# A two-layer image kernel: transposed scan output and norm in the first layer, transposed softplus and folded convolution in the second

## Chip, cores and metric

The kernel runs on one core of one Trainium2 chip. The time is the device time of one execution in microseconds (us); lower is better. The engines are named as the profile names them: PE (TensorE, matrix products; PEld is its loading of weights), DVE (VectorE), ACT (ScalarE), POOL (GpSimd) and SP (SyncE, which here only issues DMAs). Each engine works through its own queue in order. All data is float32.

## The reference, cut to what matters

The input is x of shape (8, 192, 64, 64). Layer 0 is a gated two-dimensional scan, layer 1 a pair of selective state-space scans over 4096 tokens.

```python
# layer 0
x = conv1x1(x, W_in)                                  # 192 -> 384 channels
x = depthwise_conv3x3(x, W_dw) + b_dw
x_proxy = conv1x1(x, W_xd)                            # 16 channels
ws, Ls, Us, Ds = (conv1x1(x_proxy, W) for W in (W_w, W_l, W_u, W_d))
xs = the image, its transpose, and both with the last axis flipped     # 4 directions
Gl, Gm, Gr = normalize_w(*split(ws, 3))               # each / (|Gl| + |Gm| + |Gr| + 1e-7)
# gate_scan, chunks of 8 columns, step j within a chunk:
#   h = l * x + gl * h_up + gm * h + gr * h_down
out = gate_scan(xs, Ls, Gl, Gm, Gr, 8) * Us + xs * Ds
y = sum over the 4 directions of out * w_m
y = layernorm2d(y, ln_w, ln_b)                        # over the 384 channels
y = grn(y, grn_gamma, grn_beta)                       # global response norm
x = conv1x1(y, W_out)                                 # 384 -> 192

# layer 1: xs = layernorm of x seen as (b, 4096, 192); out = xs + mamba1(xs) + mamba2(xs flipped)
xc, z = split(x @ in_w.T)                             # 384 each
xc = silu(causal_conv4(xc, conv_w) + conv_b)
dt, B, C = split(xc @ x_w.T)                          # 12, 16, 16
dt = softplus(dt @ dt_w.T + dt_b)
# over the tokens:  h = exp(dt * A) * h + dt * x * B ;  y = sum over 16 states of h * C
y = (y + D * xc) * silu(z)
return y @ out_w.T
```

## The kernel before

One core holds 128 partitions, so the 384 inner channels are three blocks (c = 0, 1, 2). Everything is unrolled, and the order in which the program issues its parts is the order of each engine's queue (`tc.manual_schedule`). The program is 512 columns wide in nearly all operations.

**Layer 0** (`tile_ss2d_kernel`) takes the 8 images one after the other. Per image:

- 24 *units* (`Image.begin`, L137, and `unit`, L188): one channel block by eight image rows. PE multiplies with W_in, ACT writes the middle tap with the bias and two side taps, POOL adds the two sides (L162), and DVE adds the six other taps (L196).
- `proxy` (L173) makes the 16-channel proxy of eight rows for the gates.
- 96 *steps* (`Step`), 3 blocks x 8 j x 4 directions d, in `scan` (L347). A step's parts run over several steps of the loop (L361 to L385), which issues parts of the steps s3, s2, s1, s0 and of the one ahead. PE makes the gates with 16 rows of contraction (L237): lam, gl, gm and gr in `gates`, and the pair of bypass and output gates in `up` (L305). DVE forms three products with the neighbours' state (`neighbour`, L263), the sum of magnitudes (`norm`, L278), two operations that refine a reciprocal made by ACT (`newton`, L294 and L295), the weighting (`mix`, L299) and the output product (`output`, L319): nine operations. POOL multiplies the entry (L257), adds a pair (L267), makes the state (L303) and multiplies the bypass dx (L313). PE adds q's terms through an identity (L273), and adds hu and dx of all four directions into one bank, yp, through an identity (`add`, L321, matmul L329). For direction 2 dx is not added by PE: POOL adds it to the dx of direction 3 (L315). After direction 3, ACT stores yp (L339). For j = 0 the state is the entry product alone, so that a step has only entry, bypass and output.
- The y of an image lies with channels on the partitions, 512 positions to a column block j. `Norm` (L388) of the image before is issued between the first units: means over the channels by a product with a constant matrix (L399), centring on DVE (L404), squares on ACT (L408), a second product (L413), an inverse root with three DVE refinements (L419 to L423), scaling on POOL (L442), and the squares' sums for the response norm on ACT (L430).
- `project_out` (L460) multiplies with W_out in 16 products (L499), spread over the later units by the list PARTS, and stores to DRAM (mid).

PSUM banks of layer 0 come from `bank` (L62): one each for gl, gm, q and yp, two for gr, two for c. The gates lam, bypass and output all take c; a tile that finds no free one waits for the last reader of an earlier one.

**Layer 1** (`tile_mamba_kernel`) has 64 blocks of 512 tokens, two *passes* for each (the two mambas), 128 in all. A pass has 24 *groups*: three channel blocks by eight pairs of states. For a group:

- `inputs` (L861): POOL multiplies dtx with the pair's rows of B, which a DMA has spread over the partitions (b_sb), into hs.
- `decays` (L867): ACT writes exp(dt * a) into a PSUM pair da, twice, and the first column of hs (L870).
- `scan` (L875): DVE runs the recurrence over 1024 columns.
- `weigh` (L882): the product with C (c_sb). DVE does it, except for *far* groups, n in FAR, whose scan is written to hs and whose product is POOL's.
- `keep` (L878): ACT saves the last state; `sum` (L887): PE adds both states' products, transposed, into yp with 8 matmuls in transpose mode.

The loop over slots (L984 to L1009) issues, at slot n: what `before[n]` lists, the inputs of group n + 3, scan n, far product n - 1, sums of n - 3 (far: n - 4), product and keep of n, decays of n + 2, and what `behind[n]` lists. The lists are made by L907 to L947. They hold the next pass's preparation: in_proj into xr (`enter`, L683), the convolution by four diagonal matrices (`convolve`, L700), z by `gate` (L712), `silu` (L721), `low_rank` (L727), the write of B and C to DRAM (bc, L735) and their 16 spread loads (`spread`, L743). `step` (L746) makes the softplus in six ACT operations with channels on the partitions; `refine` (L763) finishes it on POOL with three operations and forms dtx with a fourth (L766, L768, L770, L773); `head` makes the first column. Banks of layer 1: two for all preparation, two for yp, and two pairs for da. hs has 10 buffers, b_sb and c_sb eight each.

Of the kernel before, what the change touches and what calls it, by code (L numbers as in the profile page):

```python
# [8 lines left out]
F32 = mybir.dt.float32  # L9
# [22 lines left out]
FAR = (0, 12, 15, 20)  # L32
ACT_SET = "natural_log_exp_and_others"
JOINED = 2
UNITS = NC * CHUNK

PARTS = [0] * 8 + [1, 1, 1, 2, 1, 1, 1, 1, 1, 1, 1, 1, 1, 1, 1, 1]
# [4 lines left out]
ROWS = {GL: (0, 0), GM: (1, 0), GR: (2, 0), GLAM: (3, 0), GU: (0, 1), GD: (1, 1)}  # L42


@with_exitstack
def kernel(ctx: ExitStack, tc: tile.TileContext, x, w_in, dw, vecs, w_xd, w_gate, w_m, w_out, mid):
# [9 lines left out]
    big = ctx.enter_context(tc.tile_pool(name="l0_big", bufs=6))  # L56
# [46 lines left out]

    states = []
# [8 lines left out]
    class Image:  # L113
# [6 lines left out]
        def __init__(self, b):  # L120
            self.b = b
            self.x = x[b].rearrange("(k p) h w -> p k (h w)", p=KM)
            self.xc, self.xins, self.banks = [], {}, {}
            self.xp = p1.tile([P, CHUNK, CHUNK, HW], F32, tag="xp", name=f"xp_{b}")
            self.u = 0
            for u in range(4):
                self.load(u)
            for u in range(2):
                self.begin(u)
# [7 lines left out]
        def begin(self, u):  # L137
            c, r = divmod(u, CHUNK)
            if r == 0:
                self.xc.append(big.tile([P, HW, HW], F32, tag="big", name=f"xc_{self.b}_{c}"))  # L140
# [5 lines left out]
            self.load(u + 4)  # L146
# [26 lines left out]
        def proxy(self, r):  # L173
            pp = bank("c", f"pp_{self.b}_{r}")
# [13 lines left out]
        def unit(self):  # L188

            u, self.u = self.u, self.u + 1  # L190
            if u + 2 < UNITS:
                self.begin(u + 2)
            c = u // CHUNK
            for t in (0, 1, 2, 6, 7, 8):
                acc, part = self.shifted(u, t)
                nc.vector.scalar_tensor_tensor(  # L196
                    acc, part(self.banks[u]), dw_sb[:, c, t : t + 1], acc, ALU.mult, ALU.add
                )
            if u >= UNITS - CHUNK + 2:
                self.proxy(u % CHUNK - 2)  # L200
# [17 lines left out]
    class Step:  # L218
# [4 lines left out]
        def __init__(self, tag, xc, xp, wg, d, j):  # L223
            self.tag, self.xc, self.xp, self.wg, self.d, self.j = tag, xc, xp, wg, d, j
            self.q, self.ab = {}, {}
            self.h = states[d]
            self.hc = self.h[:, :, 1 : HW + 1]
# [4 lines left out]
        def gate(self, kind, tag):  # L232

            dst = bank(tag, f"g{kind}_{self.tag}")
            group, at = ROWS[kind]
            r = slice(32 * group, 32 * group + RANK)
            nc.tensor.matmul(dst, self.wg[r, at, self.d, :], flat(self.xp[r, self.j]), start=True, stop=True)  # L237
            return dst
# [36 lines left out]
        def norm(self):  # L275
            if self.j:
                for i in range(2):
                    nc.vector.tensor_add(self.g[2], self.g[2], flat(self.ab[i]))  # L278
# [11 lines left out]
        def newton(self):  # L290

            if self.j:
                s, rc = self.g[2], flat(self.rc)
                nc.vector.scalar_tensor_tensor(s, s, 1e-7, rc, ALU.add, ALU.mult)  # L294
                nc.vector.scalar_tensor_tensor(rc, s, 2.0, rc, ALU.subtract, ALU.mult)  # L295
# [25 lines left out]
        def add(self, i):  # L321


            if self.d == 0 and i == 0:
                self.yp = bank("yp", f"yp_{self.tag}")
            elif i == 0:
                self.yp = self.before.yp
            if i == 0 or self.d != JOINED:
                nc.tensor.matmul(  # L329
                    self.yp,  # L330
                    ident,
                    flat((self.hu, self.dx)[i]),
                    start=(self.d == 0 and i == 0),
                    stop=(self.d == ND - 1 and i == 1),
# [6 lines left out]
    class Nothing:  # L341


        def __getattr__(self, part):
            return lambda *args: None

    def scan(b, xc, xp):  # L347


        ys, steps = [], [Nothing()] * 4  # L350
        for c in range(NC):
            wg = w_gate_sb[:, :, :, c * P : (c + 1) * P]
            ys.append(big.tile([P, CHUNK, CHUNK * HW], F32, tag="big", name=f"y_{b}_{c}"))
            for j in range(CHUNK):
                steps += [Step(f"{b}_{c}_{j}_{d}", xc[c], xp, wg, d, j) for d in range(ND)]
                for step in steps[-ND:]:
                    step.y = ys[c][:, j, :]
        for before, step in zip(steps[4:], steps[5:]):
            step.before = before
        steps += [Nothing()] * 4  # L360
        for s3, s2, s1, s0, ahead in zip(steps, steps[1:], steps[2:], steps[3:], steps[4:]):  # L361
            s2.state()
            s0.neighbour(2)
            s0.neighbour(0)
            s0.entry()
            s1.newton()
            s1.total()
            s0.neighbour(1)
            s0.pair()
            s0.magnitude(2)  # L370
            s2.direct()
            ahead.gates()
            s0.norm()
            s0.log()
            ahead.decay()
            s2.bypass()
            s3.add(0)
            s2.output()
            s3.add(1)
            ahead.magnitude(0)  # L380
            s1.up()
            s0.exp()
            s1.mix()
            ahead.magnitude(1)
            s3.store()  # L385
        return ys

    class Norm:  # L388


        def __init__(self, b, ys):
            self.b, self.ys = b, ys
            self.ss = p1.tile([P, NC, CHUNK], F32, tag="ss", name=f"ss_{b}")
            self.pm, self.squares, self.var, self.rstd = {}, {}, {}, {}

        def mean(self, j):
            self.pm[j] = bank("gr", f"pm_{self.b}_{j}")
            for c in range(NC):
                nc.tensor.matmul(self.pm[j], mean_w, self.ys[c][:, j, :], start=(c == 0), stop=(c == NC - 1))  # L399

        def center(self, j):
            for c in range(NC):
                y = self.ys[c][:, j, :]
                nc.vector.tensor_sub(y, y, self.pm[j])  # L404
                sq = self.squares[j, c] = p2.tile(
                    [P, T], F32, tag=("ab0", "ab1", "dx")[c], name=f"sq_{self.b}_{j}_{c}"
                )
                nc.scalar.activation(sq, y, AF.Square)  # L408

        def variance(self, j):  # L410
            self.var[j] = bank("c", f"pv_{self.b}_{j}")
            for c in range(NC):
                nc.tensor.matmul(self.var[j], mean_w, self.squares[j, c], start=(c == 0), stop=(c == NC - 1))  # L413

        def root(self, j):

            r = self.rstd[j] = p2.tile([P, T], F32, tag="rc", bufs=3, name=f"rstd_{self.b}_{j}")
            v = self.var[j]
            nc.scalar.activation(r, v, AF.Ln, bias=eps5)  # L419
            nc.scalar.activation(r, r, AF.Exp, scale=-0.5)  # L420
            nc.vector.scalar_tensor_tensor(v, v, 1e-5, r, ALU.add, ALU.mult)
            nc.vector.tensor_mul(v, v, r)
# [665 lines left out]
```

## Time and profile before

| | us |
|---|---|
| median of 3 runs | 16998.98 (16979.7 to 17001.8) |
| the profiled execution, its own time | 16973.27 |
| its span, first to last instruction | 16971.4 |
| busy: PE | 14236.2 (84%) |
| busy: DVE | 15279.7 (90%) |
| busy: ACT | 12149.0 (72%) |
| busy: POOL | 15186.0 (89%) |

An engine is busy while one of its instructions runs; matmuls overlap, so a full PE row says that the queue never ran dry, not that the array was at its peak. The profile cuts the span into 40 slices of 424 us. Layer 0 fills the first 14 of them. The costliest groups are POOL's inputs (7157.5 us in 3072 instructions of 2357 ns) and DVE's scans (5852.3 and 1168.8 us, 2286 ns each).

### The profile page before, as it was taken

The page shows a single profiled execution, that of the slowest core. Times are in us where ns is not written, and L with a number is a line of the kernel's source. Part 1 is how long each engine was busy: PE and PEld are TensorE (multiplying, and loading weights), DVE is VectorE, ACT ScalarE, POOL GpSimd, SP SyncE. Part 2 cuts the span into 40 slices and gives each one's busy share as a digit, 9 for nine tenths or more (in the row PEclk, how much of TensorE's full clock was granted, in tenths as well). Part 3 has the DMA queues.
Part 4 walks back from the last instruction along what each step waited for, and adds up shares of the span by engine and source line. Part 5 has one row for each costly group of instructions (what it writes and reads, how often), then busy time and mean ns, then how long its engine had stood idle before and what let it go on. Part 6 is the DMA issues. An engine that isn't in the chain of part 4 may idle for free.

```text
span 16971.4 us, 183983 instructions
## 1 busy us (share of the span) xinstructions
PE 14236.2 (84%) x58320; PEld 7740.8 (46%) x58320; DVE 15279.7 (90%) x14474; ACT 12149.0 (72%) x25963; POOL 15186.0 (89%) x9955
## 2 busy tenths in 40 slices
PE   9999999999999977777777777777777777777777
PEld 2333333333333345555555555555555555555555
DVE  8888888888887779999999999999999999999999
ACT  5656666666666667777777777777777777777777
POOL 7787978778787779999999999999999999999999
PEclk8999999999999988888888888888888888888888
DMA  1001010010100022222222222222222222222222
GB/s 30 24 7 30 1 30 8 23 30 1 30 1 26 2 96 105 105 105 105 104 106 104 106 104 106 104 106 104 106 104 106 104 106 104 106 104 106 104 103 87
DMA packets 695519, 1249.43 MB, mean 74 GB/s; under 512 B 311768, under 2 KB 378672, under 8 KB 694544
## 3 DMA queue, kind: packets, MB, share of 16 engines
q1 hardware_dynamic: 694144, 1237.37, 19.9%
q8 instruction: 461, 7.55, 0.2%
q14 instruction: 514, 4.21, 0.1%
q10 hardware_dynamic: 400, 0.29, 0.0%
HBM read 1178.77 MB, written 58.72 MB: 73 GB/s over the span
## 4 chain that ended last, share of the span: by engine, by line
POOL 23%; DVE 15%; DMA 9%; ACT 8%; issue 6%; PE 4%; SPq 0%; DVEq 0%; POOLq 0%; ACTq 0%
POOL hs L861 15%; DVE da L875 11%; DMA c_sb<-bc 8%; ACT da L867 3%; POOL hs L882 3%; DVE hs L882 3%; POOL lg L768 1%; POOL e L766 1%; POOL dt L770 1%; PE pz L712 1%; POOL dtx L773 1%; DMA b_sb<-bc 1%; PE pc L700 1%; PE dbl_ps L731 1%; PE yp L887 1%
## 5 line engine op out<-in xcount | busy, mean ns | idle before, releaser
L861 POOL TENSOR_TENSOR hs<-dtx,b_sb 128x1022 f32<-128x1022 f32 x3072 | 7157.5, 2357 | 61.3 <-DMA b_sb<-bc 35.2
L875 DVE TENSOR_TENSOR_SCAN da<-da,hs 128x1024 f32<-128x1024 f32 x2560 | 5852.3, 2286 | 421.6 <-ACT hs L870 391.2
L867 ACT ACTIVATE da<-dt,a 128x512 f32<-128x512 f32 x6144 | 4247.9, 691 | 182.6
L887 PEld LDWEIGHTS yp<-ident,hs 128*128 128x128 f32 x24576 | 3022.9, 150 | 1000.1 <-issue 743.0
L887 PE MATMUL yp<-ident,hs 128*128 128x128 f32 x24576 | 3353.4, 287 | 67.1 <-DVE hs L882 59.8
L882 DVE TENSOR_TENSOR hs<-da,c_sb 128x1024 f32<-128x1024 f32 x2560 | 3129.2, 1222 | 88.7
L237 PE MATMUL g<-xp,w_gate_sb 16*128 16x512 f32 x8640 | 1812.6, 657 | 60.5 <-ACT dx L310 51.6
L700 PE MATMUL pc<-xr,conv_diag 128*128 128x512 f32 x3072 | 1542.8, 627 | 182.8 <-ACT dt L756 162.5
L878 ACT COPY state<-da 128x2 f32<-128x2 f32 x2560 | 400.8, 157 | 1626.0 <-DVE hs L882 1617.1
L820 PE MATMUL po<-out_w,z 128*128 128x192 f32 x3072 | 828.3, 420 | 748.2 <-ACT xc L704 365.3
L263 DVE TENSOR_TENSOR q<-g,h 128x512 f32<-128x512 f32 x2016 | 1353.7, 685 | 113.2 <-PE g L237 68.6
L273 PE MATMUL q<-q,ident 128*128 128x512 f32 x2688 | 1333.1, 618 | 0.0
L875 DVE TENSOR_TENSOR_SCAN hs<-da,hs 128x1024 f32<-128x1024 f32 x512 | 1168.8, 2283 | 143.1 <-ACT hs L870 87.4
L283 ACT ACTIVATE rc<-g,eps 128x512 f32<-128x512 f32 x672 | 462.2, 688 | 1119.2 <-DVE g L278 1119.2
L678 PE MATMUL pi<-xT,in_w 96*128 96x512 f32 x1536 | 955.2, 760 | 317.3 <-ACT z L812 312.2
L313 POOL TENSOR_TENSOR dx<-dx,xc 128x512 f32<-128x512 f32 x768 | 1079.7, 1406 | 155.2 <-ACT dx L310 132.7
L882 POOL TENSOR_TENSOR hs<-hs,c_sb 128x1024 f32<-128x1024 f32 x512 | 1206.7, 2357 | 1.8 <-ACT state L878 1.6
L712 PE MATMUL pz<-in_w,xT 96*128 96x384 f32 x2048 | 849.6, 541 | 421.3 <-ACT y L843 231.9
L237 PEld LDWEIGHTS g<-xp,w_gate_sb 16*128 16x128 f32 x8640 | 493.5, 188 | 1304.9 <-DVE q L263 395.9
L820 PEld LDWEIGHTS po<-out_w,z 128*128 128x128 f32 x3072 | 653.0, 245 | 829.6 <-ACT xc L704 395.3
L267 POOL TENSOR_TENSOR q<-q,q 128x512 f32<-128x512 f32 x672 | 853.6, 1270 | 193.7 <-DVE q L263 188.1
L257 POOL TENSOR_TENSOR lam<-lam,xc 128x512 f32<-128x512 f32 x672 | 942.1, 1402 | 32.1 <-ACT lam L254 32.1
(145 smaller groups left out, 25264.4 us busy)
## 6 DMA issues: line engine op xcount, KB each, us to landing
b_sb<-bc SPq DMA_DIRECT2D x1024, 512.0 KB, 9.1
c_sb<-bc SPq DMA_DIRECT2D x1024, 512.0 KB, 8.9
xin<-in_x_dram SPq DMA_DIRECT2D x192, 384.0 KB, 3.6
mid<-ot SPq DMA_DIRECT2D x128, 192.0 KB, 2.1
xt<-mid SPq DMA_DIRECT2D x64, 384.0 KB, 10.0
out_dram<-y SPq DMA_DIRECT2D x64, 384.0 KB, 2.6
bc<-dbl SPq DMA_DIRECT2D x128, 64.0 KB, 1.6
b<-bc SPq DMA_DIRECT2D x128, 8.0 KB, 7.3
```

The source lines that it names most:

```text
L237: nc.tensor.matmul(dst, self.wg[r, at, self.d, :], flat(self.xp[r, self.j]), start=True, stop=True)
L263: nc.vector.tensor_mul(self.q[i], rows(self.g[i]), self.h[:, :, i : i + HW])
L273: nc.tensor.matmul(self.sum, ident, flat(term), start=(i == 0), stop=(i == 1))
L313: nc.gpsimd.tensor_mul(self.dx, self.dx, direction(self.xc, self.d, self.j))
L700: nc.tensor.matmul(pc, self.m.conv_w[:, c, t, :], self.xr[c][:, t : t + T], start=(t == 0), stop=(t == 3))
L712: nc.tensor.matmul(pi, self.tokens.xT[:, i, s * P : (s + 1) * P], self.m.in_w[:, i, CI:], start=(i == 0), stop=(i == 1),)
L820: nc.tensor.matmul(self.po[:, s, :], self.z[:, 2 * half + s, c * P : (c + 1) * P], self.m.out_w[:, c, :], start=(c == 0), stop=(c == NC - ...
L861: nc.gpsimd.tensor_mul(self.hs[:, :, 1:], dtx, self.p.b_sb[self.g][:, :, 1:])
L867: nc.scalar.activation(self.da[:, n, :], self.p.dt[self.c], AF.Exp, scale=self.p.m.a[:, self.c, at : at + 1])
L875: nc.vector.tensor_tensor_scan(h, da, hs, 0.0, ALU.mult, ALU.add)
L882: engine.tensor_mul(self.hs, self.h, self.p.c_sb[self.g])
L887: nc.tensor.matmul(self.p.yp[self.c][:, s, :], self.hs[:, n, s * P : (s + 1) * P], ident, is_transpose=True, start=False, stop=(self.g == ...
```

## The change

**Layer 0.** hu and dx of every direction are added to yp by four matmuls in transpose mode each, so that yp and y come out with positions on the partitions and channels along the row. POOL no longer joins two dx. y lies in one tile for all blocks. The norm uses the engine's row statistics, and `back` transposes the scaled y again for the output product.

```diff
-            if self.d == JOINED + 1:
-                nc.gpsimd.tensor_add(self.dx, self.dx, self.before.dx)
...
-            if i == 0 or self.d != JOINED:
+            term = flat((self.hu, self.dx)[i])
+            for s in range(BLOCKS):
                 nc.tensor.matmul(
-                    self.yp,
+                    self.yp[:, s, :],
+                    term[:, s * P : (s + 1) * P],
                     ident,
-                    flat((self.hu, self.dx)[i]),
+                    is_transpose=True,
...
+        def stats(self, j):
...
+            for s in range(BLOCKS):
+                st = p2.tile([P, 6], F32, tag="st", name=f"st_{self.b}_{j}_{s}")
+                nc.vector.bn_stats(st, yT[:, j, s, :])
+                nc.vector.bn_aggr(self.mv[pair][:, j % 2 * BLOCKS + s, :], st)
+        def root(self, pair):
...
+            nc.scalar.activation(r, v, AF.Ln, bias=eps5)
+            nc.scalar.activation(r, r, AF.Exp, scale=-0.5)
+            nc.gpsimd.tensor_scalar_add(v, v, 1e-5)
...
+        def scale(self, j):
+            for s in range(BLOCKS):
+                y, at = yT[:, j, s, :], j % 2 * BLOCKS + s
+                nc.gpsimd.tensor_scalar(
+                    y, y, self.rstd[j // 2][:, at : at + 1], self.mv[j // 2][:, at, 0:1], ALU.mult, ALU.add
+                )
+        def back(self, j):
...
+                for s in range(BLOCKS):
+                    nc.tensor.transpose(pt[:, s * P : (s + 1) * P], yT[:, j, s, c * P : (c + 1) * P], ident)
...
+                nc.scalar.copy(y_of[c][:, j, :], banks[c])
+                nc.scalar.activation(sq, banks[c], AF.Square, ...)
```

The order comes from lists of slots: every part of unit u, step k or norm j is issued at its own number plus a constant, all sorted. An image takes 128 slots: 24 units, 4 empty ones, 96 steps, 4 empty ones. The output products (`project`) stand at slots 12.3 to 31.25, the last three after the first gates. Some of a step's constants:

```diff
+STEP_PLAN = {
+    "neighbour 0": 0.04,
+    "neighbour 1": 0.12,
+    "newton 0": 1.12,
+    "total": 1.14,
+    "newton 1": 1.16,
+    "add 0": 3.19,
+    "norm 0": 0.2,
+    "gates": -0.76,
+    "add 1": 3.3,
+    "norm 1": 0.41,
+    "mix": 1.46,
+    "neighbour 2": -0.49,
+    "up": 1.53,
+    "output": 2.69,
+    "direct": 1.86,
+    "state": 1.98,
...
+}
```

**Layer 1.** xT has 128 + 64 rows with the last 64 twice, shifted by one token, and three columns of the tokens before; the convolution's taps are multiplied into W_in at the start, so that six matmuls make a block of xc, and `enter` and its copies go. The softplus is made with tokens on the partitions: four matmuls (the bias is a row of the weights), six ACT operations in three parts, then 16 transposes add the four terms into pj, and ACT copies dt out. POOL keeps only dtx.

```diff
+            taps = [(0, 0), (0, 1), (0, 2), (0, 3), (1, 1), (1, 3)]
+            for n in range(3 * part, 3 * part + 3):
+                k, at = taps[n]
+                nc.tensor.matmul(self.pc[c], w[:, n, :], x[:, k, at : at + T], start=(n == 0), stop=(n == 5))
...
+                nc.scalar.activation(w, e, AF.Identity, bias=1.0)
+                nc.scalar.activation(lg, e, AF.Ln, bias=1.0)
+                nc.scalar.activation(w, w, AF.Identity, bias=1.0, scale=-1.0)
+            else:
+                pj = bank(f"pj_{self.tag}_{c}")
+                for s in range(T // P):
+                    for i, term in enumerate(self.terms[c]):
+                        nc.tensor.matmul(pj[:, s * P : (s + 1) * P], term[:, s, :], ident, is_transpose=True, ...)
+                d = self.dt[c] = p2.tile([P, T], F32, tag="dt", name=f"dt_{self.tag}_{c}")
+                nc.scalar.copy(d, pj)
+        def weighted(self, c):
+            dtx = self.dtx[c] = p2.tile([P, T], F32, tag="dtx", name=f"dtx_{self.tag}_{c}")
+            nc.gpsimd.tensor_mul(dtx, self.dt[c], self.xc[:, c, :])
```

Eight groups of a pass are far, and the order is again a sorted list of slots, with a pass at every 24:

```diff
-FAR = (0, 12, 15, 20)
+FAR = (1, 2, 9, 10, 13, 14, 19, 22)
+PASS_PLAN = {
...
+    "silu": [
+        (-6.87, ()),
+    "low_rank": [
+        (-5.74, ()),
+    "spread": [
+        (-5.6, (0, 0)), (-5.1, (1, 0)), (-4.6, (0, 1)), (-4.1, (1, 1)), ...
+    "step": [
+        (-4.71, (0, 0)), (-4.5, (0, 1)), (-4.26, (0, 2)), (-3.4, (0, 3)), (-1.98, (1, 0)), ...
+    "weighted": [
+        (-2.72, (0,)), (2.72, (1,)), (10.16, (2,)),
...
+GROUP_PLAN = {
+    "inputs": -2.27,
+    "decay 0": -1.27,
+    "start": -1.22,
+    "decay 1": -1.18,
+    "scan": 0.02,
+    "weigh": 0.44,
+    "keep": 0.7,
+    "sum": 3.21,
+}
+FAR_PLAN = GROUP_PLAN | {"weigh": 1.64, "keep": 0.47, "sum": 4.15}
```

Tokens are loaded by two DMAs, the second for the doubled 64 channels. Layer 1's set-up loads W_in's left half in pieces, with the taps spread over the partitions, and multiplies them on DVE (4 x 2 products for each half and mamba); the bias row of dt_w comes in three small DMAs.

More of the change, by code (lines that the diff above doesn't have):

```diff
@@ L122, in __init__ @@
             self.x = x[b].rearrange("(k p) h w -> p k (h w)", p=KM)
[L123 to L129, printed above, removed]
+            self.xc = [xc_all[:, c] for c in range(NC)]
+            self.xins, self.banks = {}, {}
+            self.xp = None
         def load(self, u):
@@ L339, in store @@
                 nc.scalar.copy(self.y, self.yp)
[L341 to L386, printed above, removed]
@@ L388 @@
-    class Norm:
[L391 to L418, printed above, removed]
@@ L907, with at @@
+    def at(slot, part, *args):
+        plan.append((slot, len(plan), part, args))
     for n, p in enumerate(passes):
[L908 to L917 removed]
```

697 lines of the change are left out of this document (364 added, 333 removed), and 6 rows, old and new, of tables (NORM_PLAN, PASS_PLAN).

## The prediction

> **What bounds the kernel now.** I read the page's slices first, then busy time in 20 us windows, the timeline of one step and of one pass, the groups by line, and the waits. The slices show two layers.
>
> ```profile
> PE   9999999999999977777777777777777777777777
> DVE  8888888888887779999999999999999999999999
> POOL 7787978778787779999999999999999999999999
> PEclk8999999999999988888888888888888888888888
> ```
>
> Layer 0 (to 5971 us, where layer 1's first load is issued) looks bound by PE, layer 1 by POOL and DVE together. The windows (span, then PE, PEld, DVE, ACT, POOL busy, clock, DMA) split layer 0:
>
> ```profile
> 500.00:520.00 20.00, 18.01 (x38) 5.31 (x36) 4.60 (x7) 4.71 (x9) 13.27 (x10) 0.83 0.00 0
> 600.00:620.00 20.00, 20.00 (x72) 6.51 (x74) 19.64 (x33) 14.11 (x27) 19.59 (x16) 1.00 0.00 1
> 740.00:760.00 20.00, 15.72 (x30) 6.28 (x29) 13.23 (x20) 13.33 (x26) 9.77 (x8) 0.83 0.08 20
> 820.00:840.00 20.00, 20.00 (x48) 8.27 (x47) 18.47 (x27) 12.89 (x17) 9.39 (x8) 1.00 0.27 76
> ```
>
> In order: the change of channel block (j = 0), steady steps, units with the norm, units with the output projection. In steady steps PE is full, but DVE is 98% full as well: relief on PE alone can win 2% there. One step on PE:
>
> ```profile
> 2005.29 1.98 PE L273 MATMUL q<-q,ident 128*128 128x512 f32 x4
> 2007.21 1.14 PE L237 MATMUL g<-xp,w_gate_sb 16*128 16x512 f32 x8
> 2008.28 1.13 PE L329 MATMUL yp<-hu,ident 128*128 128x512 f32 x2
> 2009.24 1.02 PE L329 MATMUL yp<-dx,ident 128*128 128x512 f32 x2
> 2010.19 1.13 PE L237 MATMUL g<-xp,w_gate_sb 16*128 16x512 f32 x4
> 2011.25 1.98 PE L273 MATMUL q<-q,ident 128*128 128x512 f32 x4
> ```
>
> Start to start: 1.92, 1.07, 0.96, 0.96, 1.06, in all 5.96 us; 4.98 for d = 2, which has no dx product: 5.72 on average. DVE's nine operations fill 98% of that, 5.61. For layer 1, one pass:
>
> ```profile
> 9016.08 9.32 POOL L861 TENSOR_TENSOR hs<-dtx,b_sb 128x1022 f32<-128x1022 f32 x4
> 9018.88 0.58 ACT L733 COPY dbl<-dbl_ps 44x512 f32<-44x512 f32 x1
> 9025.37 1.26 POOL L766 TENSOR_TENSOR e<-e,w 128x512 f32<-128x512 f32 x1
> 9029.40 1.28 POOL L773 TENSOR_TENSOR dtx<-dt,xc 128x512 f32<-128x512 f32 x1
> 9030.76 2.35 POOL L861 TENSOR_TENSOR hs<-dtx,b_sb 128x1022 f32<-128x1022 f32 x1
> ```
>
> and what POOL and DVE waited for from 6200 to 16800 us:
>
> ```profile
> POOL mv L639 <- ACT rstd L633: 114.9, 61, 2.8
> POOL e L766 <- ACT state L878: 57.3, 57, 3.3
> POOL rest L788 <- ACT rest L785: 42.6, 43, 2.7
> POOL hs L861 <- DMA b_sb<-bc: 33.6, 63, 2.5
> DVE da L875 <- ACT hs L870: 385.6, 291, 2.4
> ```
>
> The writes of bc run from 6026.5 to 16860.1 us, 127 passes of 85.3. POOL per pass: 24 inputs at 2.32 (four in 9.29) 55.7, 4 far products at 2.33 9.3, 12 operations of refine and dtx at 1.34 (9025.37 to 9030.76 is four) 16.1, small ones 2.4: 83.5. Its waits, 250 us over 124 passes, are the other 2.0. DVE: 20 near groups at 3.46 (scan and product), 4 far at 2.20, 3.1 of others: 81.1. So POOL sets the pass.
>
> **The change, part by part.**
>
> *Full steps.* The 8 transposes that replace hu's and dx's products cost what 8 cost in layer 1, 0.88 us (9006.75 to 9007.63). PE per step becomes 1.92 + 1.07 + 1.06 + 0.88 = 4.93. POOL loses the join (1.27 us in one step of four). DVE stays at 5.61, so that is the low bound. The high bound is a loop in the new order: pu takes the bank that output frees, and output now stands on DVE behind neighbour 2, which waits for the gates. Around it: pu 0.96, total 1.92, half the transposes 0.44, gates 1.07, neighbour 2 0.60, output 0.68, hand-overs 0.2 (0.09 from gate to copy at 2000.26, twice): 5.9. Queued behind pu are the next total and gates, and DVE's mix waits for those. Between 5.61 and 5.9 I take 5.72, the row of before: 0. Over 84 steps x 8 images the bounds are -74 and +121 us.
>
> *The j = 0 steps* (12 an image) are not held by DVE (4.60 of 20). PE saves 1.68 - 0.88 = 0.8 in each: 0.8 x 96 = -77; bounds 0 and, if order hides the drain too, -150.
>
> *Units, norm and output.* The last store to the first gate is 2164 to 2338, 174 us, of which 76 carry the norm (2164 to 2240), one j in 8.4: DVE six taps 4.45, centre 1.87, root 2.1. Removed are centring, root, squares and two mean products. Added on DVE are 4 bn_stats and 4 bn_aggr a j: 192 elements take 0.335 and 0.182; 384 by the same rate 0.54 + 0.18, 2.9 a j. Eight units and eight j then need 35.6 + 23.2 = 59 on DVE; POOL 8 x 2.4 for sides, 32 scales (no row; between 0.23, the smallest tensor_scalar, and 0.95, 3/4 of a 512 product; I take 0.95) and four roots of 1.5: 56; ACT's copies and squares 24 x 1.6 + 16 + 3: 57. With filling I take 62, -14. The later 98 us are PE's: 15 units at 1.88, 16 + 8 products at 2.58: 90. Three of the 16 move under the first steps: 82 and little waiting, -14, of which the steps give back 3. Per image -25, seven times -175; bounds 0 and -280, since three engines fill together. The SP stores move with them and wait for nothing new. The tail after the last image (5850 to 5971) loses its serial chain of 9 us a j: -15; bounds 0, -30.
>
> *Layer 1, POOL.* Nine refine operations go (12.0), four products come (9.3), dtx stays at 1.28: 80.5. DVE loses 4 x 1.26: 76.1. PE gains 48 transposes at 0.11, 5.3, in a pass where it is 77% busy; the convolution is 36 instructions of 512 before (24 + 12) and after. ACT loses the copies of xr (2.8) and gains 1.7 of dt copies and some halos. POOL remains the bound, with DVE 4 us below it, which was its stall on ACT before (3.7 a pass). What is late next is dtx of the first block. From silu (9011.54) POOL had 13.8 us of work before refine; inputs could begin 19.2 after silu, when dtx and b_sb were both there (b_sb lands 9.1 after its issue at 9021.56, 30.7). The new order leaves four inputs and one far product, 11.6, before dtx, which should start at 17.9: a shortfall of 6.3 if POOL keeps step with ACT. It need not: inputs are issued 2.27 slots (7.6 us) ahead of their scan, and an engine that is the bound falls behind by about that. So the new stall lies between 0 and 6.3; nearest is a POOL that runs late: 1.2. Waits that stay (newton, rest, b_sb) are 1.5. The pass: 80.5 + 1.5 + 1.2 = 83.2, -2.1 x 127 = -267; bounds 81.0 (-546) and 88.3 (+381).
>
> *Set-up* of layer 1: 26 more DMA issues on SP at 0.45, products of 0.3 on DVE beside them: +15; bounds 0, +30. Of moved transfers, xt's second load goes out at slot 10.7 of a pass and out_dram's store at 1.6, when SP has no loads of b and c to issue but the last; those 16 keep their half-slot pitch and go out behind bc as before. Neither is on the way to a scan: 0.
>
> *Sum*: 0 - 77 - 175 - 15 - 267 + 15 = -519 on the profiled execution's own 16973.3 (span 16971.4): 16454. The median of the runs shown, 16999.0, is 26 above that execution, their lowest 6 above; I add 16 and say 16470.
>
> [...] Steady steps show a clock of 1.00, and layer 1, where transposes already run, 0.87 to 0.90, falling after PE waits. [...] Likewise a far product takes 2.36 us on POOL against 1.22 on DVE. [...]
>
> **Rivals.** *Both bounds fall*: steps at 5.61, the order hides the drains, POOL waits 0.5: -74 - 110 - 225 - 15 - 510 + 15 = -919, 16050. For it: DVE at 98% in steady steps; against: the chain through b_sb. *The bank loop*: steps 5.9 and the units no shorter: +121 - 77 - 267 + 15 = -208, 16765. For it: DVE's order; against: banks may be given out otherwise. *Slower, by b_sb*: POOL stands before dtx and inputs in every pass. Layer 0 and set-up bring -252, so it decides from 2.0 us above 85.3, a stall of 5.3; at 6.3 the pass is 88.3, +129, 17100. For it: POOL already waits there in 63 of 124 passes; against: POOL can run late.
>
> **How the numbers follow.** Forecast 0.50 (own range 16230 to 16700), both bounds 0.22, bank loop 0.12, slower 0.16. Within 0.2%, which is about what a measurement here tells from no change, only the tail of the bank loop falls: 0.03; 0.01 of it is slower. Faster 0.80, slower 0.17. The range 16000 to 16950 takes in the first two and the third.
>
> **What would show it.** Steady steps: PE near 86%, a step of 5.6 to 5.9; if over, PE waiting for output's product is the loop. Units: below 160 us. A pass of 83, POOL over 96%, its largest wait at dtx or the first inputs. Wrong if the clock falls in the steps, if POOL waits over 5 us a pass, or if DVE's stalls on ACT pass 7.

## The result, and the profile after

The changed kernel takes 18157.05 us (median of 4 runs, 18116.89 to 18177.62) against 16989.34 us (4 runs): 1.0685 times as long, 95% interval 1.0664 to 1.0706. It is slower; the prediction said 16470, and faster. The profiled execution has a span of 18157.5 us. Three lines of its page say where to look (40 equal slices of the span, tenths):

```profile
PE   9999999999999999888888888888888888888888
DVE  6666666676767666599999999999999999999999
PEclk7776767676767676799999999999999999999998
```

Layer 0 now fills 16 to 17 slices instead of 14, DVE has fallen from 8 to 6 there, and the clock granted to PE from 9 to 6 or 7. Layer 1, in contrast, is as full as before. Dated by the first load of layer 1, by the first and last write of bc, and in layer 0 by DVE's output products hu (to 2 us), the two spans differ so:

| us | before | after | difference |
|---|---|---|---|
| steps of an image, first to last hu, mean of 8 | 550.5 | 769.5 | +219 x 8 = +1752 |
| between two images' hu, mean of 7 | 185.1 | 166.0 | -19.1 x 7 = -134 |
| up to the first hu; last hu to layer 1 | 144; 127 | 148; 96 | +4; -31 |
| layer 1's first load | 5971.2 | 7562.5 | **+1591** |
| from there to the first write of bc | 55.3 | 71.8 | +16.5 |
| 127 passes, by the writes of bc | 85.30 each | 82.03 each | **-416** |
| last write to the end | 111.3 | 105.8 | -5.5 |

So all parts but one went the way they should; the full steps lost more than the rest won. Windows cut at the changes of the clock show how (window, its length, PE, PEld, DVE, ACT, POOL busy, granted clock, DMA):

```profile
1099.50:1110.00 10.50, 10.25 (x45) 4.30 (x44) 8.75 (x14) 5.81 (x12) 8.22 (x8) 0.99 0.00 0
1110.00:1117.00 7.00, 7.00 (x18) 2.58 (x16) 3.92 (x7) 1.44 (x3) 5.02 (x4) 0.52 0.00 0
1117.00:1120.00 3.00, 2.87 (x13) 1.02 (x9) 1.89 (x3) 2.54 (x6) 1.39 (x2) 1.00 0.00 0
1120.00:1123.50 3.50, 3.50 (x6) 1.33 (x6) 3.19 (x5) 1.57 (x4) 1.91 (x2) 0.53 0.00 0
1219.00:1263.50 44.50, 44.50 (x101) 18.32 (x100) 26.39 (x42) 16.89 (x32) 24.33 (x19) 0.50 0.00 1
```

In this trace PE has the full or half the clock, nothing between, for stretches of about 3.4, 7, 10.5 us and so on: multiples of 3.4. The last line's stretch at half lasts 44 us, with PE busy all the time; the longest in this trace's steps lasts 75 us (from 1301). In before, 173 of the 216 windows of 20 us that lie in the steps have a clock of 1.00; in after none of 303 has, and the mean is 0.68. The same step, once at full and once at half clock (start, duration, instruction):

```profile
1099.98 0.60 PE L466 MATMUL yp<-ident,hu 128*128 128x128 f32 x4
1100.51 1.14 PE L376 MATMUL g<-xp,w_gate_sb 16*128 16x512 f32 x8
1101.58 0.66 PE L466 MATMUL yp<-ident,dx 128*128 128x128 f32 x4
1102.36 1.96 PE L376 MATMUL g<-xp,w_gate_sb 16*128 16x512 f32 x4
1104.25 1.98 PE L412 MATMUL q<-q,ident 128*128 128x512 f32 x4
1106.07 0.49 PE L466 MATMUL yp<-ident,hu 128*128 128x128 f32 x3
...
1233.75 1.06 PE L466 MATMUL yp<-ident,hu 128*128 128x128 f32 x4
1234.74 2.09 PE L376 MATMUL g<-xp,w_gate_sb 16*128 16x512 f32 x8
1236.76 1.11 PE L466 MATMUL yp<-ident,dx 128*128 128x128 f32 x4
1237.81 2.65 PE L376 MATMUL g<-xp,w_gate_sb 16*128 16x512 f32 x4
1240.38 3.78 PE L412 MATMUL q<-q,ident 128*128 128x512 f32 x4
1243.95 1.06 PE L466 MATMUL yp<-ident,hu 128*128 128x128 f32 x4
```

Start to start, 6.09 us and 10.2 us. At full clock the pair of L376 takes 1.89 us from start to start instead of the 1.06 of before: its two products wait for a bank, one after the other:

```profile
1102.36 0.29 PEld L376 LDWEIGHTS g<-xp,w_gate_sb 16*128 16x128 f32 x2 [0.36 <-ACT lam L393]
1102.40 0.68 DVE L455 TENSOR_TENSOR hu<-g,h 128x512 f32<-128x512 f32 x1
1103.20 0.29 PEld L376 LDWEIGHTS g<-xp,w_gate_sb 16*128 16x128 f32 x2 [0.55 <-issue]
```

The first begins once ACT has copied lam, the second 0.12 us after the output product hu is done (e11's lines below name that wait). That is the loop which the prediction priced at 5.9.

### The profile page after: what moved, and what is told of

Read it like the earlier page. It is cut to its first block, busy times and chain, and to the rows that moved or that the text cites. A ratio compares the mean times of both kernels' runs of the same rounds, so it can differ in the third digit from the quotient of the medians.

```text
span 18157.5 us, 206099 instructions
## 1 busy us (share of the span) xinstructions
PE 16479.7 (91%) x70224; PEld 9701.3 (53%) x70224; DVE 14689.6 (81%) x14098; ACT 11578.6 (64%) x25411; POOL 14686.7 (81%) x9388
## 4 chain that ended last, share of the span: by engine, by line
POOL 19%; PE 11%; ACT 10%; DVE 8%; issue 6%; DMA 4%; SPq 0%; POOLq 0%; DVEq 0%; ACTq 0%
POOL hs L979 13%; DVE da L995 5%; POOL hs L1002 5%; PE pc L801 4%; ACT da L985 3%; DMA b_sb<-bc 3%; PE pz L811 2%; PE yp L1007 2%; DVE hs L995 2%; PE pj L880 2%; DVE hs L1002 1%; DMA c_sb<-bc 1%; POOL dtx L893 1%; ACT xc L822 1%; ACT z L823 1%
## 5 line engine op out<-in xcount | busy, mean ns | idle before, releaser
L995 DVE TENSOR_TENSOR_SCAN da<-da,hs 128x1024 f32<-128x1024 f32 x2048 | 4686.6, 2288 | 416.6 <-POOL hs L979 322.1
L376 PE MATMUL g<-xp,w_gate_sb 16*128 16x512 f32 x8640 | 2955.2, 844 | 63.1 <-ACT lam L393 2.4
L995 DVE TENSOR_TENSOR_SCAN hs<-da,hs 128x1024 f32<-128x1024 f32 x1024 | 2314.3, 2280 | 317.9 <-ACT da L985 228.8
L1002 DVE TENSOR_TENSOR hs<-da,c_sb 128x1024 f32<-128x1024 f32 x2048 | 2499.9, 1221 | 62.2 <-DVE da L995 0.5
L1002 POOL TENSOR_TENSOR hs<-hs,c_sb 128x1024 f32<-128x1024 f32 x1024 | 2418.8, 2362 | 3.8 <-ACT state L998 3.8
L801 PE MATMUL pc<-xT,conv 128*128 128x512 f32 x4608 | 2173.6, 605 | 71.2 <-ACT xT L774 69.1
L412 PE MATMUL q<-q,ident 128*128 128x512 f32 x2688 | 2171.2, 954 | 0.0
L396 POOL TENSOR_TENSOR lam<-lam,xc_all 128x512 f32<-128x512 f32 x672 | 941.2, 1401 | 539.2 <-ACT lam L393 524.7
L801 PEld LDWEIGHTS pc<-xT,conv 128*128 128x128 f32 x4608 | 817.0, 192 | 988.8 <-issue 864.4
L441 POOL TENSOR_TENSOR h<-lam,rc 128x512 f32<-128x512 f32 x672 | 853.5, 1270 | 540.1 <-DVE rc L437 536.5
L376 PEld LDWEIGHTS g<-xp,w_gate_sb 16*128 16x128 f32 x8640 | 858.5, 238 | 798.1 <-issue 480.9
L451 POOL TENSOR_TENSOR dx<-dx,xc_all 128x512 f32<-128x512 f32 x768 | 1074.5, 1399 | 71.4 <-ACT dx L448 70.4
## 6 DMA issues: line engine op xcount, KB each, us to landing
b_sb<-bc SPq DMA_DIRECT2D x1024, 512.0 KB, 10.2
```

Of the source, the lines that this page charges most:

```text
L376: nc.tensor.matmul(dst, self.wg[r, at, self.d, :], flat(self.image.xp[r, self.j]), start=True, stop=True)
L396: nc.gpsimd.tensor_mul(self.lam if self.j else self.hc, self.lam, direction(self.xc, self.d, self.j))
L412: nc.tensor.matmul(self.sum, ident, flat(term), start=(i == 0), stop=(i == 1))
L801: nc.tensor.matmul(self.pc[c], w[:, n, :], x[:, k, at : at + T], start=(n == 0), stop=(n == 5))
L995: nc.vector.tensor_tensor_scan(h, da, hs, 0.0, ALU.mult, ALU.add)
L1002: engine.tensor_mul(self.hs, self.h, self.p.c_sb[self.g])
```

## The experiments

Each is told by when layer 1 begins (5971 before, 7562 after) and by the clock in the steps: its mean, and how many of the 20 us windows have 1.00. One run each, but for the last version.

**What pulls the clock down: transposes, the loop, or too little work?** e1 and e2 edit after, e3 and e4 edit before.

```diff
# e1
-                    is_transpose=True,
# e2
-    "output": 2.69,
+    "output": 2.45,
# e3, in before
-                nc.tensor.matmul(self.yp, ident, flat((self.hu, self.dx)[i]), ...)
+                term = flat((self.hu, self.dx)[i])
+                for s in range(4):
+                    nc.tensor.matmul(self.yp[:, s * P : (s + 1) * P], term[:, s * P : (s + 1) * P], ident, is_transpose=True, ...)
...
# e4, in before
-            if i == 0 or self.d != JOINED:
+            if i == 0 and self.d in (0, ND - 1):
...
```

> The kernel after, with the eight transposes of a step in layer 0 run as plain products (stationary the term's 128 columns, moving the identity): same blocks, same order, same layout of y. Theory 1, transposes do not hold the full clock: the products give back the work that holds it, the clock of the steady steps goes from 0.50 to 0.91 back to 0.95 or more, PE pays about 1.0 us more a step than with transposes, so the step is the bank loop's 6.09 us plus up to 0.5, and layer 1 begins between 6100 and 6600 us (7562 after, 5971 before). Theory 2, the loop through output and its pauses on PE lets the clock fall: the pauses stay, the clock goes on falling to 0.50, layer 1 begins later than 7200 us. Theory 3, less matrix work in a step of whatever kind: as theory 1. Layer 1 as in after: 82.0 us a pass.

> The kernel after, with only the slot of output moved from 2.69 to 2.45, so that on DVE it stands behind the norm, ahead of mix and of the next step's neighbour 2; the loop through pu's bank no longer holds the gates. Theory 2: the step at full clock falls from 6.09 to 5.6 to 5.75 us, the clock stays at 0.95 or more, layer 1 begins at 5700 to 5950 us. Theories 1 and 3: stretches at 0.50 remain, layer 1 begins at 7200 to 7560 us, and only the steps at full clock are shorter.

> The kernel before, with only the products of hu and dx in layer 0 run as four transposes of 128 columns each (seven terms of a row of four steps as before; y then lies transposed in its blocks, so the norm and the output are computed on another layout with the same instructions). DVE's order is that of before, with output ahead of mix. Theory 1: the clock of the steps falls to 0.5 in stretches and layer 1 begins later than 6900 us. Theory 2: clock 0.95 or more as before, steps of 5.6 us, layer 1 begins at 5800 to 5950 us. Theory 3: as theory 1. Layer 1 as in before: 85.3 us a pass.

> The kernel before, with the products of hu and dx in layer 0 left out except that of hu for the first and the last direction: y lacks the other terms. No transposes; plain products of 0.96 us in a step fall from 1.75 to 0.5 on average, so PE has 4.5 us of plain work in a step, 0.45 more than after. Theory 1: the clock stays at 0.95 or more, steps are DVE's 5.6 us, layer 1 begins at 5750 to 5950 us. Theory 3, the clock follows the amount of matrix work: it falls to 0.5 in stretches, layer 1 begins later than 6500 us. Theory 2 expects the same as theory 1.

| | us | layer 1 begins | clock in steps | at 1.00 |
|---|---|---|---|---|
| e1 | 17018.4 | 6436 | 0.95 | 204 of 248 |
| e2 | 16578.0 | 5982 | 0.885 | 47 of 224 |
| e3 | 17075.3 | 6077 | 0.88 | 74 of 219 |
| e4 | 17451.2 | 6443 | 0.75 | 0 of 240 |

No theory fits all four. In e1 the loop is still there (steps of 6.5 us) and the clock is back, which fells theory 2 alone. In e2 one place in DVE's queue takes 1581 us off, with all transposes in place, though its 5982 misses theory 2's 5950 as well, and e3 has transposes and loses only 105: theory 1 expected far more. And e4 has no transpose and no loop, has less to do than before, and is 471 us later:

```profile
1040.00:1060.00 20.00, 19.20 (x55) 6.58 (x55) 17.98 (x30) 12.28 (x24) 15.64 (x12) 0.84 0.00 1
```

Something like theory 3 is left: the clock goes by how much PE does, and it remains to be found what counts.

**Do transposes count?** Both edit e2: e5 keeps two of eight terms, e6 issues every transpose twice.

```diff
# e5
+            for s in range(BLOCKS if (self.d, i) in ((0, 0), (ND - 1, 1)) else 0):
# e6
+            for n in range(2 * BLOCKS):
+                s = n % BLOCKS
...
```

> The kernel after with output first (slot 2.45), and of each eight terms of y only the first and the last transposed; y lacks the other six. PE keeps the 4.05 us of plain products a step and loses three quarters of its transposes; what they filled becomes a pause. Transposes count for nothing: the plain share of PE's time is that of the run with output first, so are the clock (some single dips, 0.91 to 1.00 in steps, mean of layer 0 about 0.9) and the begin of layer 1, 5900 to 6050 us. Transposes count as work: PE is some 75% occupied, less than in the run of before with few adds (6442 us), and layer 1 begins later than 6500 us.

> The kernel after with output first, and each transpose of layer 0 issued twice into the same bank, so that y is twice as large. PE's work is 4.05 of plain products and 2.1 us of transposes in a step: no pause is left, the step cannot be under 6.15, and the plain share is 66%, that of the kernel after at full clock (4.05 of 6.09). Transposes count for nothing: the clock falls to 0.50 in stretches as in after, layer 1 begins later than 7000 us. Transposes count as work: clock 0.97 or more, steps of 6.2 us, layer 1 begins at 6150 to 6350 us.

e5: 16910.3 us, layer 1 at 6321, clock 0.755, none of 240 windows at 1.00. e6: 16600.8, layer 1 at 6014, clock 0.955, 183 of 224. First a window of e5, then two of e6:

```profile
1800.00:1820.00 20.00, 18.67 (x44) 5.88 (x48) 17.37 (x29) 10.42 (x21) 16.35 (x13) 0.67 0.00 0
```

```profile
1680.00:1700.00 20.00, 20.00 (x113) 10.31 (x111) 18.86 (x31) 11.46 (x23) 17.42 (x15) 1.00 0.00 1
1700.00:1720.00 20.00, 20.00 (x113) 10.39 (x109) 18.89 (x32) 13.36 (x26) 17.68 (x14) 1.00 0.01 1
```

With as little plain work as after, e6 holds 1.00 through its steps. Transposes count, and taking them away costs the clock: e5 begins layer 1 at 6321, 339 us after e2, though not past the 6500 expected. e6 came earlier than the 6150 expected, since its step is 5.94 us and not 6.15.

**Other fillers, and the loop with a full PE.** e8 makes hu's four blocks plain in e2; e10 adds two transposes of zeros behind dx in e2; e9 is after, loop and all, with every transpose twice.

```diff
# e8
+                    is_transpose=i == 1,
# e10
+            terms = [term[:, s * P : (s + 1) * P] for s in range(BLOCKS)] + [nought] * (2 * i)
...
```

> The kernel after with output first, hu's four blocks as plain products (0.98 us for four), dx's as transposes (0.53). PE has 5.03 us of plain work and 0.53 of transposes in a step that DVE holds at 5.5 to 5.6. If the dips of the run with output first come from too little plain work, the clock is 0.97 or more in the steps and layer 1 begins 100 to 250 us earlier, at 5730 to 5880 us, in all 16330 to 16480. If they come from the order or the pauses at j = 0, the clock stays at 0.91 to 1.00 and layer 1 begins at 5950 to 6020.

> The kernel after in its own order, loop and all, with each transpose of layer 0 issued twice into the same bank, so that y is twice as large. The loop through pu's bank grows by half a term's transposes to 6.5 us; PE has 6.1 us to do in it. If the clock falls because PE stands idle or does too little in a step, it stays at 0.97 or more, the steps are 6.4 to 6.6 us and layer 1 begins at 6350 to 6550 us: earlier than in after (7562) though PE has more to do. If the loop itself pulls the clock down, stretches at 0.50 stay and layer 1 begins later than 7000 us.

> The kernel after with output first, and behind dx's four transposes two more, of a tile of zeros, added into the same bank: they change no value and fill the pause of 0.22 to 0.35 us in which PE waits for output. Occupancy decides: the clock in full steps rises from 0.93 to 0.97 or more, the step stays at DVE's 5.5 to 5.6 us, layer 1 begins at 5850 to 5930 us (5982 without), in all 16440 to 16530. If the clock follows something else, such as the rows of the array in use or the data in it: clock 0.90 to 0.96 as before, layer 1 begins at 5960 to 6030.

e8: 16678.3 us, layer 1 at 6084, 1.00 in 124 of 229 windows. A miss of both: the clock rose only in part (a mean of 0.91 in the steps, 47 windows to 124), and the step grew from 5.5 to 5.8 us. e9: 16970.2, layer 1 at 6374, 208 of 245 at 1.00: the loop does not pull the clock down when PE has enough to do, and after with *more* work on PE is 1187 us faster. e10: 16332.2, layer 1 at 5747, 162 of 212, better than the 5850 to 5930 expected.

**Rows of the array.** What tells e2 (0.885) from before (0.96) is not idle time: PE is 97% busy in e2. But 2.1 us of each step are gates, products over 16 of 128 rows. e11 edits e2 so that they run over 32 rows at the same duration; e15 does so with zeros in the added rows.

```diff
+    nc.gpsimd.memset(w_gate_sb, 0.0)
...
-        nc.sync.dma_start(w_gate_sb[32 * group : 32 * group + RANK, at], w_gate[:, kind])
+        for half in (0, RANK):
+            first = 32 * group + half
+            nc.sync.dma_start(w_gate_sb[first : first + RANK, at], w_gate[:, kind])
+    nc.vector.tensor_scalar_mul(w_gate_sb, w_gate_sb, 0.5)
...
-            r = slice(32 * group, 32 * group + RANK)
+            r = slice(32 * group, 32 * group + 2 * RANK)
```

> The kernel after with output first, and the gates' products on 32 rows instead of 16: the rows of xp and of the gates' weights stand twice and the weights are halved, so the products and their times are the same. Occupancy decides: nothing changes, clock 0.93 in full steps, layer 1 begins at 5970 to 6010 us (some 10 us of more loads at the start). If the clock counts rows of the array in use (a gate with 16 of 128 rows next to nothing), the clock rises to 0.97 or more and layer 1 begins at 5800 to 5930.

> The kernel after with output first and the gates' products on 32 rows, of which 16 hold zeros in the weights and in xp. If rows addressed count: as with wide gates, clock 1.00 in full steps, layer 1 begins at 5580 to 5610 us. If only rows with data that change count: as without, 5960 to 6000 us.

e11: 16184.1 us, layer 1 at 5592, 181 of 207 windows at 1.00, over 200 us earlier than expected, with no pause filled and no instruction of the steps added. e15: 16181.4 and 5587, 182 of 207: zeros do as well. One step and one window of e11 (its window shows PE as idle as in e2):

```profile
1902.34 0.60 PE L472 MATMUL yp<-ident,hu 128*128 128x128 f32 x4
1902.87 1.30 PE L382 MATMUL g<-xp,w_gate_sb 32*128 32x512 f32 x8
1904.10 0.66 PE L472 MATMUL yp<-ident,dx 128*128 128x128 f32 x4
1904.98 1.13 PE L382 MATMUL g<-xp,w_gate_sb 32*128 32x512 f32 x4 [0.22 <-DVE hu L461]
1906.03 1.98 PE L418 MATMUL q<-q,ident 128*128 128x512 f32 x4
```

```profile
1640.00:1660.00 20.00, 19.11 (x92) 8.80 (x90) 19.79 (x34) 12.63 (x25) 19.11 (x15) 1.00 0.00 1
```

DVE is 99% busy: it sets this step of 5.57 us.

**Clock and loop apart.** e13 is after with the wide gates alone, e14 with the two fillers of e10 too; output stays at 2.69.

> The kernel after in its own order, loop and all, with the gates' products on 32 rows instead of 16 (rows of xp and of the weights twice, weights halved). Theory R, each 3.4 us window is decided by array rows times time: counting full rows as 1, transposes included, the share of a step was 0.68 in before, 0.63 to 0.72 in the runs that kept 1.00, 0.59 with output first (0.93), 0.53 in after; here (1.92 + 1.06 + 0.25 x 2.13) / 6.06 = 0.58, just under: clock 0.85 to 0.97, no stretches of 40 us at 0.50, layer 1 begins at 5900 to 6300 us. Theory L, the loop's pauses alone decide: as in after, layer 1 begins later than 7000.

> As e13, and two transposes of a tile of zeros behind dx's: share (1.92 + 1.32 + 0.53) / 6.09 = 0.62. Theory R: clock 0.98 or more in full steps, the loop alone is left: steps of 6.06 to 6.12 us, an image's steps 560 to 570 us, layer 1 begins at 5880 to 5960 us, in all 16480 to 16560. Theory L: stretches at 0.50, later than 7000.

e13: 16718.6 us, layer 1 at 6118, 144 of 232 windows at 1.00. e14: 16627.1, layer 1 at 6032, 198 of 224, steps of an image 577.5 instead of 769.5. One step of e14:

```profile
1802.45 1.14 PE L384 MATMUL g<-xp,w_gate_sb 32*128 32x512 f32 x8
1803.52 0.66 PE L475 MATMUL yp<-ident,dx 128*128 128x128 f32 x4
1804.01 0.38 PE L475 MATMUL yp<-ident,nought 128*128 128x128 f32 x2
1804.33 2.13 PE L384 MATMUL g<-xp,w_gate_sb 32*128 32x512 f32 x4
1806.38 1.98 PE L420 MATMUL q<-q,ident 128*128 128x512 f32 x4
```

The pair still takes 2.05 us for 1.06 of work: the loop at full clock, steps of 6.2 us, which is more than e14 was expected to take (6.06 to 6.12, layer 1 from 5880 to 5960). So of after's layer 0, mending the clock first takes off 7562 - 6032 = 1530 us, and the loop then 6032 - 5592 = 440 us, e14 to e11 (e11 has no fillers, and no need of them). In the other order the same 1970 us or so are 1581 for the loop's place (e2) and 390 for the wide gates (e11): the two are not independent.

**The version that mends both.** e16 is e11 again, in five rounds; e17 is before with the wide gates.

> The kernel after with output first and wide gates again, timed: 16184 us against 16975 to 16990 before, ratio 0.9520 to 0.9540. Theory R and every other that explains the first run expect the same; it tells only whether that run can be repeated.

> The kernel before with the gates' products on 32 rows (rows of xp and of the weights twice, weights halved), nothing else. Theory R: its full steps already have 1.00 and stay at 5.72 us; only the twelve steps of an image with j = 0, now at 0.77 to 0.88, come to 0.95 or more: 10 to 20 us an image, layer 1 begins at 5810 to 5890 us instead of 5971, layer 1 unchanged, in all 16820 to 16910. Theory L: nothing changes, 16960 to 17000.

e16: 16184.39 us, 0.9531 times before (0.9518 to 0.9544): faster than both kernels. e17: 16884.7 us (before beside it 16976.0), layer 1 at 5878, steps of an image 539 instead of 550.5.

**The second layer.** e7 joins before's layer 0 to after's layer 1; e12 is e2 with four far products.

```diff
# e12
-FAR = (1, 2, 9, 10, 13, 14, 19, 22)
+FAR = (1, 9, 13, 19)
```

> The whole first layer of before with the whole second layer of after. The two layers do not meet in time but at the set-up, so the time is the sum of their parts: layer 1 begins at 5971 us, set-up 72 us instead of 55, passes of 82.0 us instead of 85.3: 16970 + 17 - 416 = 16571 for the span. A rival is that layer 1's passes gained from what layer 0 left behind (clock, SBUF addresses): then the passes are 83 or more and the span above 16690.

> The kernel after with output first and FAR cut to (1, 9, 13, 19): four of 24 products with C on POOL as before the change, twenty on DVE. By rows POOL then has 80 - 9.4 = 71 us a pass and DVE 76 + 4 x 1.26 = 81 us and its stalls of 3 to 4: passes of 83 to 85 us instead of 82.0, in all 16700 to 16950 (16578 with eight). [...]

e7: 16566.0 us (span 16564.2), layer 1 from 5973: the layers add up. e12: 16991.6, passes of 85.3 us, (16878.7 - 6045.5) / 127, both a little over their ranges. DVE, at 94%, sets them, and POOL has room:

```profile
8000.00:8500.00 500.00, 434.60 (x2290) 313.73 (x2289) 470.68 (x306) 370.21 (x876) 413.35 (x239) 0.89 0.29 108
```

The whole gain of layer 1, 3.3 us a pass, hangs on the four more products on GpSimd: without them the new softplus and convolution bring nothing. The reverse, four more products with the old softplus, was not run; by the prediction's rows POOL, full at 83.5 us a pass, had no room for their 9.3. Such a product takes 2362 ns on POOL and 1221 on DVE, and moving four more is right all the same, since DVE was the dearer place: 85.3 us a pass with four on POOL (e12), 82.0 with eight.

## Why the prediction was wrong

**Full steps: the step that failed.** It said "I take 5.72, the row of before: 0", with bounds of -74 and +121 us, and the steps grew by 1752 us (its -77 for j = 0 lies in them too). Two errors lie in it.

- *The clock.* The durations of before's steps were taken from rows with a granted clock of 1.00, as if that belonged to the operation. It went with the mix: a mean of 0.96 in before's steps, of 0.68 in after's. The prediction reckoned that adds of 1.68 us a step would become transposes of 0.88 (1.02 in after's lines), called that PE's gain, and put the fall of the clock that this brought at nothing since before's steps read 1.00; it named such a fall only as a sign of being wrong. Take as a step's share the time that PE spends on products over all 128 rows, transposes with them, and a quarter of the time on 32 rows, over the length of the step at full clock (durations as in the lines above; a measure of mine, not the chip's):

| run | share | windows at 1.00 |
|---|---|---|
| e6, before | 0.66, 0.63 | 0.82, 0.80 |
| e11, e14, e1, e9 | 0.62, 0.61, 0.61, 0.60 | 0.87, 0.88, 0.82, 0.85 |
| e8, e10, e13 | 0.59, 0.59, 0.56 | 0.54, 0.76, 0.62 |
| e2, e3, after | 0.53, 0.50, 0.48 | 0.21, 0.34, 0 |
| e4, e5 | 0.44, 0.37 | 0, 0 |

  At 0.60 or more every run has 1.00 in at least 0.80 of its windows, at 0.59 or less in at most 0.76. Before, at 0.63, stood little above that; for after, (1.92 + 0.53 + 0.49) / 6.09 = 0.48. The weights were chosen after most of these runs, though e13 and e14 were forecast by them. Rows of 16 counted as an eighth order the runs less well. How narrow products are to be weighed stays open: the four of `gates` run side by side (8 records in 1.14 us, where the pair's 4 take 1.13), and counting the rows that they cover together (64 of 128, and 128 in e11) orders the runs nearly as well.

  The records of single stretches say more than these averages. Cut the steps on the grid of 3.41 us on which the clock changes (in before and after all 2350 stretches of one clock, but the last of each, are whole multiples of it), and take from each window the share in which a product over 128 rows runs, transposes with them. In the eleven runs with gates on 16 rows (before, after, e1 to e6, e8 to e10) the next window's clock goes by it nearly always, but for a band between:

| clock in the window | share of 128-row products | windows | next one changes |
|---|---|---|---|
| 1.00 | under 0.25 | 727 | 723 fall |
| 1.00 | 0.25 to 0.40 | 1984 | 414 fall |
| 1.00 | 0.40 or more | 8557 | 6 fall |
| 0.50 | under 0.60 | 2135 | 0 return |
| 0.50 | 0.60 to 0.80 | 595 | 195 return |
| 0.50 | 0.80 or more | 1013 | 1009 return |

  In e11, with gates on 32 rows, only 5 of 51 windows under 0.25 are followed by a fall. So in these runs one window under 0.25 was enough to lose the full clock (723 of 727), and one of 0.80 or more nearly always brought it back (1009 of 1013), one of 0.60 to 0.80 in a third of the cases (195 of 595). In after (the gates alone: window, length, their PE time, clock, DMA; PE is busy all the time at half clock):

```profile
1246.47:1249.89 3.42, 2.44 (x8) 0.50 0.00 0
1249.89:1253.30 3.41, 0.77 (x2) 0.50 0.00 0
1253.30:1256.71 3.41, 1.56 (x8) 0.50 0.00 0
1256.71:1260.13 3.42, 2.44 (x8) 0.50 0.00 0
1260.13:1263.54 3.41, 0.73 (x2) 0.50 0.01 2
1263.54:1266.95 3.41, 1.75 (x10) 1.00 0.00 0
1266.95:1270.37 3.42, 1.35 (x4) 1.00 0.02 5
1270.37:1273.78 3.41, 2.48 (x11) 1.00 0.00 0
1273.78:1277.19 3.41, 1.62 (x2) 0.50 0.00 0
```

- *The loop.* Its place was right, down to pu, output and neighbour 2, and it was given 0.12. Its price, 5.9, was low: 6.09 in after at full clock, 6.2 in e14. The two errors feed each other: a longer step has a smaller share, and at half clock the loop's own products stretch (eight of L376 take 2.09 us instead of 1.14).

**What the prediction said of the clock.** It added up the steps at the clock of the rows, and the two readings that it named didn't bear on that: a clock of 1.00 in steps without transposes says nothing on steps with them, and layer 1's 0.87 to 0.90 was put down to PE's waits untested. Transposes alone did not lower it: e6 has 1.00 in 183 of 224 windows with about 2 us of each step in transposes.

**Steps with j = 0** (-77). In after they lie within the lost steps and can't be told apart. Before's ran at 0.77 to 0.88; e17 gets 11.5 us an image from them by the clock alone.

**Units, norm, output** (-175). Right in kind: -134, 166 us from hu to hu instead of 185, the same in every run with the new layer 0 but for 2 us. **Tail** (-15): -31. **Set-up** (+15): +16.5.

**Layer 1** (-267, a pass of 83.2). Right, and too careful: 82.03, -416. POOL was to be busy for 80.5 and wait for 2.7. It was busy for 486.3 of 500 us on average of three windows, 79.8 a pass, and waited 220 us in some 123 passes, 1.8 each, at the two places named:

```profile
POOL hs L979 <- DMA b_sb<-bc: 115.4, 135, 2.7
POOL dtx L893 <- ACT state L998: 84.6, 91, 1.7
POOL hs L979 <- PE yp L1007: 10.2, 10, 2.9
```

**Sum.** With the clock held but the loop in place (e14), the changed kernel takes 16627: inside the range, between the forecast and the rival of the loop. With both mended it is 16184, 801 us under before, while the wide gates alone take only 91 off before (e17). The change had more in it than the -519 of the forecast; the clock and the loop took it.

**Open.** Why after stands at half clock for up to 75 us at a time, where the longest stretch in the steps is 34 us in e4 and 24 in e5, with smaller shares. The windows above suggest it: after's step at half clock, 10.2 us, is nearly three windows, so that windows cut every step at nearly the same places, and the fullest of the three creeps from 0.77 to 0.80 before the clock returns. A step of another length at half clock was not tried for this. The loop leaves a pause in PE there too (2.57 us for a pair of 2.0), which was not tested apart. Open as well is what decides in the two bands between (414 of 1984 fall, 195 of 595 return), and how narrow products enter.

## What to carry to other kernels

A duration on PE holds only at the clock of the row it comes from (1.14 us at full, 2.09 at half, for the same eight products): before work is taken from PE, add up what share of a step uses all its rows, look for stretches of 3.4 us that hold little of it (under 0.25, 723 of 727 were followed by a fall here), and ask what the clock does there. Products over few rows could be widened here at no time (the pair takes 1.13 us on 16 rows and on 32), and with zeros as well as with data (e15 16181.4 us, e11 16184.1). And where a product waits for a bank, follow the bank around its loop at both ends; one place in a queue was worth 440 us here at full clock, and 1581 with the clock that it pulled along.

## What was not expected of the hardware

- In the traces of before and after the granted clock is 1.00 or 0.50, in stretches of 3.41 us and multiples of it up to 249 us.
- The clock rose with the rows that a product addresses: going from 16 to 32 of 128 in e2's gates, with data or zeros, takes the windows at 1.00 from 47 of 224 to 181 or 182 of 207 and brings 394 to 397 us, though no product gets shorter by itself (the pair takes 1.13 us in e8 and e11) and PE's pauses stay.
- In these runs the full clock was lost and regained at different shares: at full clock, 6 of 8557 windows with 0.40 or more of 128-row products are followed by a fall; at half clock, none of 2135 with under 0.60 by a return.
- PE's row may read busy throughout, as over 44.5 us of after, and the clock still be half.
- With fp32 transposes, each issued twice, the steps of e6 have 1.00 in 183 of 224 windows, with plain products in their place those of e1 in 204 of 248; four blocks cost 0.53 us as transposes, 0.98 plain.
